# Sigmoid attention over 96x96 images: two key chunks per step of the attention loop instead of three

## The chip, the cores and the metric

The kernel runs on one core of a Trainium2 chip. A core has a matrix engine (TensorE, PE in the profile; its weight loads are listed as PEld), a vector engine (VectorE, DVE), an engine for activation functions (ScalarE, ACT), a general one (GpSimd, POOL) and one that mostly issues DMA transfers (SyncE, SP). The engines run their own instruction queues in order and wait for one another through semaphores. TensorE writes its results into PSUM, a memory of eight banks, each 512 fp32 numbers wide per partition; ScalarE and VectorE read them from there.

The metric is the device time of one execution in microseconds (us).

## The reference

The input x has the shape (4, 64, 96, 96): four images b, 64 channels, N = 9216 positions. Two layers are applied, each to a group-normalized copy of x and added to x:

```python
Q = (wq @ gn(x) + bq)          # 8 channels, per image
K = (wk @ gn(x) + bk)          # 8 channels
V = (wv @ gn(x) + bv)          # 64 channels
energy = einsum('bcn,bcm->bnm', Q, K)        # 9216 x 9216 per image
att = sigmoid(energy)
out = einsum('bcm,bnm->bcn', V, att) + gn(x)
x = x + out * channel_gate(out)              # gate from mean and maximum of each channel
# second layer: a spectral convolution with few frequencies
x = x + irfft2(lowpass_mix(rfft2(gn(x))))
```

There is no softmax: the attention matrix is a sigmoid of each energy, so the sum over keys m can be cut into chunks of any size.

## The kernel before

**Tiling.** Two images form a pair: 2 x 64 channels fill the 128 partitions. The loop over p runs over the two pairs. Positions are cut in blocks of NB = 512 (NBLK = 18) for queries, and in chunks of P = 128 (NCH = 72) for keys.

**Per pair.** First come group statistics (`group_stats`) and then the projection of keys and values: for each of the 18 blocks s, VectorE normalizes 512 columns (`normalize`, L135), TensorE computes the keys (L163, one matmul) and the transposed values (L166, four matmuls) into one PSUM tile `proj`, ScalarE makes two copies of the keys with bias (L171, L172), VectorE joins these into `kT` (L177, four instructions, one for each key chunk) and copies the values into `vT` (L180). The keys stand four times in the 128 partitions, as four groups of 32 rows: two images, times two.

**The attention loop.** For each query block n an accumulator `acc` in PSUM is summed over all keys. A step t takes three key chunks, so there are NT = 24 steps in a block. `energies(n, t, q)` issues six matmuls (L207): three chunks times two images, each with 32 rows of weights from `kT` and 512 query columns from `q`. The row group of a matmul is r = 32 * (2 * (m % 2) + b), so that the first four matmuls use four different groups and the last two use the first two groups again. The results fill two PSUM tiles of three banks each. ScalarE applies the sigmoid to each tile with one instruction of 1536 columns (L212) and writes `at` to SBUF. `values(acc, t, ats)` issues six matmuls (L220) with 64 columns of weights, one image in each half of the array's columns; the profile lists twelve records for them, as each is done in two passes. In the program order the energies of step t + 1 stand ahead of the values of step t, so that ScalarE can work meanwhile.

**Queries.** `project_q(n + 1)` (L191, then L195 to L197 on VectorE) is called after the values of step NT - 3 of block n; its result is first used by the energies that are issued in step NT - 1.

**Buffers.** PSUM: pool `ps_s` has two slots of three banks, used by `proj` and by the energies `e`; pool `ps_a` has two slots of one bank for `acc`, `pq` and small things. In SBUF the pool `att` has four slots for `at` and, in the projection, `kk` (the two copies of the keys); the pool `q` holds `q`, `qh` and `ql`. With these slots the first energies of a step wait until the first sigmoid of the step before has read its PSUM tile, and the fourth energy matmul waits for the second sigmoid.

**After the loop** the channel gate is computed, x is updated (L265), and after the second pair the spectral stage follows. Its four constant matrices fw, fh, gh and gw are loaded by ScalarE's DMA queue at its start (L280 to L283).

The order of the work on each engine follows the program text, except that a scheduler moves independent instructions, such as the normalization of later blocks, forward or back.

Of the kernel before, what the change touches and what calls it, by code (L numbers as in the profile page):

```python
# [13 lines left out]
F32 = mybir.dt.float32  # L14
F32R = mybir.dt.float32r
AF = mybir.ActivationFunctionType
ALU = mybir.AluOpType
AX = mybir.AxisListType
PSUM = bass.MemoryType.PSUM

P = 128
B, C, H, W = 4, 64, 96, 96
# [4 lines left out]
KW = 16  # L27
KH = 32
NB = 512
NBLK = N // NB  # L30
NCH = N // P
NT = NCH // 3
WKH = 2
GN_EPS = 1e-5

# [2 lines left out]
def tile_kernel(ctx: ExitStack, tc: tile.TileContext, x, wqT, bq, wkT, bk, wvT, bv,  # L38
                w1T, w2T, spec, fw, fh, gh, gw, pairavg, halves, out):
    nc = tc.nc  # L40
# [3 lines left out]
    const = ctx.enter_context(tc.tile_pool(name="const", bufs=1))  # L44
# [40 lines left out]
    q_low, q_sign, k_low, k_sign = (hv[:, i:i + 1] for i in range(4))  # L85
# [10 lines left out]
    for b in range(2):  # L96
# [2 lines left out]
        nc.scalar.dma_start(w2_sb[b * R:(b + 1) * R, b * C:(b + 1) * C], w2T)  # L99
        nc.scalar.dma_start(bv_sb[:, b, :], bv.to_broadcast([P, C]))  # L100

    turn = [0]

    def evacuate(dst, src):
# [29 lines left out]
    def normalize(dst, src, mr):  # L134
        nc.vector.tensor_scalar(dst, src, mr[:, 0:1], mr[:, 1:2], ALU.subtract, ALU.mult)  # L135
# [4 lines left out]
    with tc.tile_pool(name="xn", bufs=1) as xnp, \  # L140
            tc.tile_pool(name="kv", bufs=1) as kvp, \
            tc.tile_pool(name="q", bufs=2) as qp, \
            tc.tile_pool(name="att", bufs=4) as attp, \
            tc.tile_pool(name="ps_s", bufs=2, space=PSUM) as ps_s, \
            tc.tile_pool(name="ps_a", bufs=2, space=PSUM) as ps_a:
        for p in range(NPAIR):
            xt = xs[p]
# [5 lines left out]

            xn = xnp.tile([P, N], F32, tag="xn", name=f"xn_{p}")


            kT = kvp.tile([P, NT, 2, P], F32R, tag="kT", name=f"kT_{p}")
            vT = kvp.tile([P, NCH, P], F32, tag="vT", name=f"vT_{p}")
            for s in range(NBLK):
                cols = bass.ts(s, NB)  # L160
                normalize(xn[:, cols], xt[:, cols], mr)
                pp = ps_s.tile([P, 3, NB], F32, tag="s", name=f"proj_{p}_{s}")
                nc.tensor.matmul(pp[:, 0, :], wk_sb, xn[:, cols], start=True, stop=True)  # L163
                for i in range(4):
                    j = 4 * s + i
                    nc.tensor.matmul(pp[:, 1, bass.ts(i, P)], xn[:, bass.ts(j, P)], wv_sb,  # L166
                                     start=True, stop=True)

                kk = attp.tile([P, 3, NB], F32, tag="att", name=f"kk_{p}_{s}")
                kh, kl = kk[:, 0, :].bitcast(F32R), kk[:, 1, :]  # L170
                nc.scalar.activation(kh, pp[:, 0, :], AF.Identity, bias=bk_sb[:, 0:1])  # L171
                nc.scalar.activation(kl, pp[:, 0, :], AF.Identity, bias=bk_sb[:, 1:2],  # L172
                                     scale=k_low)
                for i in range(4):
                    t, m = (4 * s + i) // 3, (4 * s + i) % 3
                    rows = slice(64 * (m % 2), 64 * (m % 2) + 64)
                    nc.vector.scalar_tensor_tensor(  # L177
                        kT[rows, t, m // 2, :], kk[rows, 0, bass.ts(i, P)],
                        k_sign[rows, :], kl[rows, bass.ts(i, P)], ALU.mult, ALU.add)
                nc.vector.tensor_tensor(  # L180
                    vT[:, 4 * s:4 * s + 4, :],
                    pp[:, 1, :].rearrange("p (i m) -> p i m", m=P),
                    bv_sb.rearrange("p b c -> p (b c)").unsqueeze(1).to_broadcast([P, 4, P]),
                    ALU.add)
# [4 lines left out]
            def project_q(n):  # L189
                pq = ps_a.tile([P, NB], F32, tag="a", name=f"pq_{p}_{n}")  # L190
                nc.tensor.matmul(pq, wq_sb, xn[:, bass.ts(n, NB)], start=True, stop=True)  # L191
                qh = qp.tile([P, NB], F32R, tag="hi", bufs=1, name=f"qh_{p}_{n}")
                ql = qp.tile([P, NB], F32, tag="lo", bufs=1, name=f"ql_{p}_{n}")
                q = qp.tile([P, NB], F32R, tag="q", name=f"q_{p}_{n}")
                nc.vector.tensor_scalar(qh, pq, bq_sb[:, 0:1], None, ALU.add)  # L195
                nc.vector.tensor_scalar(ql, pq, bq_sb[:, 0:1], q_low, ALU.add, ALU.mult)
                nc.vector.scalar_tensor_tensor(q, qh.bitcast(F32), q_sign, ql, ALU.mult, ALU.add)  # L197
                return q

            def energies(n, t, q):  # L200

                es = [ps_s.tile([P, 3, NB], F32, tag="s", name=f"e_{p}_{n}_{t}_{i}")
                      for i in range(2)]
                for i in range(6):
                    m, b = i // 2, i % 2
                    r = 32 * (2 * (m % 2) + b)
                    nc.tensor.matmul(es[i // 3][:, i % 3, :], kT[r:r + 32, t, m // 2, :],  # L207
                                     q[r:r + 32, :], start=True, stop=True)
                ats = []
                for i in range(2):  # L210
                    at = attp.tile([P, 3, NB], F32, tag="att", name=f"at_{p}_{n}_{t}_{i}")
                    nc.scalar.activation(at, es[i], AF.Sigmoid)  # L212
                    ats.append(at)
                return ats

            def values(acc, t, ats):
                for i in range(6):
                    j, b = 3 * t + i // 2, i % 2
                    half = slice(b * C, (b + 1) * C)
                    nc.tensor.matmul(acc[half, :], vT[:, j, half], ats[i // 3][:, i % 3, :],  # L220
                                     start=(j == 0), stop=(j == NCH - 1))

            q = project_q(0)
            ats = energies(0, 0, q)
            for n in range(NBLK):
                acc = ps_a.tile([P, NB], F32, tag="a", name=f"acc_{p}_{n}")
                for t in range(NT):
                    nxt = None
                    if t + 1 < NT:
                        nxt = energies(n, t + 1, q)  # L230
                    elif n + 1 < NBLK:
                        nxt = energies(n + 1, 0, q)
                    values(acc, t, ats)
                    ats = nxt
                    if t == NT - 3 and n + 1 < NBLK:
                        qn = project_q(n + 1)
                    if t == NT - 2 and n + 1 < NBLK:
                        q = qn
                blk = xn[:, bass.ts(n, NB)]
                nc.vector.scalar_tensor_tensor(blk, acc, 1.0, blk, ALU.mult, ALU.add,  # L240
                                               accum_out=sums[:, n:n + 1])
                nc.vector.tensor_reduce(maxs[:, n:n + 1], blk, AX.X, ALU.max)


            f = small.tile([P, 2], F32, tag="f", name=f"f_{p}")
# [25 lines left out]
    with tc.tile_pool(name="big", bufs=1) as big, \  # L271
            tc.tile_pool(name="wspec", bufs=3) as wp, \
            tc.tile_pool(name="strip", bufs=3) as sp, \
            tc.tile_pool(name="ps1", bufs=8, space=PSUM) as ps:

        fw_sb = big.tile([W, 3 * KW], F32, tag="fw", name="fw_sb")
        fh_sb = big.tile([H, 2, 3 * KH], F32, tag="fh", name="fh_sb")
        gh_sb = big.tile([2 * KH, H], F32, tag="gh", name="gh_sb")
        gw_sb = big.tile([2 * KW, W], F32, tag="gw", name="gw_sb")
        nc.scalar.dma_start(fw_sb, fw)  # L280
        nc.scalar.dma_start(fh_sb, fh)
        nc.scalar.dma_start(gh_sb, gh)
        nc.scalar.dma_start(gw_sb, gw)  # L283

        def bank(name):
            return ps.tile([P, NB], F32, tag="b", name=name)
# [4 lines left out]
        for p in range(NPAIR):  # L291
# [12 lines left out]
            a = big.tile([H, 2, KW, 3, C], F32, tag="t24", name=f"a_{p}")  # L304
            for g in range(P // 8):
                pa = bank(f"pa_{p}_{g}")
                for i in range(8):
                    nc.tensor.matmul(pa[:H, bass.ts(i, 3 * KW)], xT[:, :, 8 * g + i], fw_sb,  # L308
                                     start=True, stop=True)
                b, c0 = 8 * g // C, 8 * g % C  # L310
# [21 lines left out]
        for g in range(KH // WKH):  # L332
            wt = wp.tile([P, WKH, KW, C], F32, tag="wt", name=f"wt_{g}")
            nc.sync.dma_start(wt.rearrange("q h k o -> q (h k o)"), spec[g])
            for i in range(WKH):
                kh = WKH * g + i
                pv = bank(f"pv_{kh}")
                for kw in range(KW):
                    nc.tensor.matmul(pv[:C, bass.ts(kw, 3 * B)], wt[:, i, kw, :],  # L339
                                     u[:, kh, kw, :, :].rearrange("q s b -> q (s b)"),  # L340
                                     start=True, stop=True)
# [3 lines left out]
        for p in range(NPAIR):  # L345
# [16 lines left out]
            for g in range(P // 4):  # L362
                pz = bank(f"pz_{p}_{g}")
                for i in range(4):
                    b, o = (4 * g + i) // C, (4 * g + i) % C
                    nc.tensor.matmul(pz[:2 * KW, bass.ts(i, H)],  # L366
                                     vt[:, b, :, :, o].rearrange("q e k -> q (e k)"), gh_sb,
                                     start=True, stop=True)
# [69 lines left out]
```

## Time and profile before

| | us |
|---|---|
| median of 3 runs | 3665.22 |
| lowest and highest run | 3664.88, 3665.68 |
| the profiled execution, its own time | 3665.68 |
| span of its profile, first to last instruction | 3663.9 |
| TensorE busy in the span | 3510.7 |
| ScalarE busy | 2535.0 |
| VectorE busy | 408.2 |
| sigmoids (L212), 1728 of 1448 ns | 2412.3 |
| values (L220), records of TensorE | 2419.8 |
| energies (L207), records of TensorE | 635.4 |
| key and value projection (L163, L166), records of TensorE | 83.3 |

The page's busy times are sums over the whole program. A matmul's record lasts from its start until its result is out, so that records of following matmuls overlap: a mean of 601 ns for a value matmul doesn't mean that TensorE needs 601 ns for each. The distance from one start to the next is what counts, and it is read from the timeline.

In time order the program has five parts: loading and statistics until 33 us; projection and attention of pair 0 until 1594; gate, update and statistics until 1621; projection and attention of pair 1 until 3160; gate, update and the spectral stage until the end.

### The profile page before, as it was taken

To read this page: it belongs to the slowest core of one execution; us is meant where nothing else is said; L and a number is where in the kernel's file an instruction comes from. 1 tells how busy PE (TensorE), PEld (TensorE's weight loads), DVE (VectorE), ACT (ScalarE), POOL (GpSimd) and SP (SyncE) were. 2 spreads that over 40 slices of the span, in tenths; PEclk is the share of its full clock that TensorE was granted. 3 is DMA by queue.
4 is the path that set the end of the run, shared out by engine and by line. 5 is a ranking of instruction groups with operands and counts; after the bars stand their busy time and mean duration, and the time that the engine had idled before them with its cause. 6 is when DMAs were issued, how large, how long until landed. Compare 5 with 4: busy or idle time off the path is not lost.

```text
span 3663.9 us, 42847 instructions
## 1 busy us (share of the span) xinstructions
PE 3510.7 (96%) x19016; PEld 1439.6 (39%) x19016; DVE 408.2 (11%) x778; ACT 2535.0 (69%) x1908; POOL 2.9 (0%) x10
## 2 busy tenths in 40 slices
PE   3999999999999999968999999999999999699999
PEld 2333333333333333323333333333333333289999
DVE  6100000000000000052000000000000000431032
ACT  1788888888888888847888888888888888411011
POOL 0000000000000000000000000000000000000000
PEclk9999999999999999989999999999999999855555
DMA  3000000000000000000000000000000000000311
GB/s 106 1 1 1 1 1 1 1 1 1 1 1 1 1 1 1 1 1 1 1 1 1 1 1 1 1 1 1 1 1 1 1 1 1 36 1 24 127 52 52
DMA packets 9705, 38.75 MB, mean 11 GB/s; under 512 B 4689, under 2 KB 4913, under 8 KB 6449
## 3 DMA queue, kind: packets, MB, share of 16 engines
q1 hardware_dynamic: 5184, 35.65, 2.7%
q8 instruction: 149, 2.44, 0.3%
q10 hardware_dynamic: 4336, 0.37, 0.1%
q14 instruction: 36, 0.29, 0.0%
HBM read 26.58 MB, written 9.44 MB: 10 GB/s over the span
## 4 chain that ended last, share of the span: by engine, by line
PE 53%; DVE 1%; issue 0%; ACT 0%; POOLq 0%; POOL 0%; DVEq 0%
PE acc L220 32%; PE e L207 8%; PE pv L339 3%; PE pa L308 2%; PE py L375 2%; PE pz L366 2%; PE pu L320 1%; PE pu L323 1%; PE pq L191 0%; DVE strip L135 0%; PE pvt L353 0%; DVE x L265 0%; DVE stats L113 0%; PE pt L300 0%; DVE xT L108 0%
## 5 line engine op out<-in xcount | busy, mean ns | idle before, releaser
L212 ACT ACTIVATE at<-e 128x1536 f32<-128x1536 f32 x1728 | 2412.3, 1448 | 554.8 <-PE e L207 553.1
L220 PE MATMUL acc<-at,vT 128*64 128x512 f32 x10368 | 2419.8, 601 | 0.0
L220 PEld LDWEIGHTS acc<-at,vT 128*64 128x64 f32 x10368 | 668.3, 136 | 1306.3 <-issue 1306.3
L207 PE MATMUL e<-q,kT 32*128 32x512 f32 x5184 | 635.4, 461 | 6.7 <-DVE vT L180 6.1
L207 PEld LDWEIGHTS e<-q,kT 32*128 32x128 f32 x5184 | 256.3, 182 | 707.3 <-issue 480.4
L195 DVE TENSOR_SCALAR qh<-pq,wqb 128x512 fp32r<-128x512 f32 x36 | 27.0, 750 | 2533.3 <-PE pq L191 2533.3
L339 PE MATMUL pv<-u,wt 128*64 128x12 f32 x1024 | 109.4, 261 | 0.0
L339 PEld LDWEIGHTS pv<-u,wt 128*64 128x64 f32 x1024 | 109.3, 227 | 0.2 <-issue 0.2
L308 PE MATMUL pa<-fw_sb,xT 96*96 96x48 f32 x512 | 84.5, 361 | 1.3 <-ACT xT L110 1.3
L308 PEld LDWEIGHTS pa<-fw_sb,xT 96*96 96x96 f32 x512 | 84.2, 257 | 1.8 <-ACT xT L110 1.8
L163 PE MATMUL proj<-xn,wk 128*128 128x512 f32 x72 | 43.1, 686 | 43.3 <-DVE vT L180 19.8
L375 PE MATMUL py<-gw_sb,z 32*128 32x96 f32 x384 | 82.5, 417 | 1.8 <-ACT z L110 1.8
L375 PEld LDWEIGHTS py<-gw_sb,z 32*128 32x128 f32 x384 | 82.1, 328 | 2.4 <-ACT z L110 2.4
L366 PE MATMUL pz<-gh_sb,vt 64*32 64x96 f32 x512 | 82.3, 364 | 0.0
L366 PEld LDWEIGHTS pz<-gh_sb,vt 64*32 64x32 f32 x512 | 81.6, 174 | 0.3 <-issue 0.3
L171 ACT ACTIVATE kk<-proj,wkb 128x512 fp32r<-128x512 f32 x36 | 24.7, 687 | 79.7 <-PE proj L166 38.8
L110 ACT COPY v<-pv 64x192 f32<-64x192 f32 x16 | 7.6, 477 | 101.4 <-PE pv L339 101.4
L110 ACT COPY z<-pz 32x384 f32<-32x384 f32 x32 | 25.4, 795 | 57.2 <-PE pz L366 57.2
L110 ACT COPY a<-pa 96x384 f32<-96x384 f32 x16 | 12.8, 799 | 73.5 <-PE pa L308 73.5
L240 DVE SCALAR_TENSOR_TENSOR xn<-acc,xn 128x512 f32<-128x512 f32 x36 | 24.9, 692 | 312.2 <-PE acc L220 312.2
L177 DVE SCALAR_TENSOR_TENSOR kT<-kk,hv 64x128 fp32r<-64x128 f32 x144 | 46.9, 345 | 26.1 <-ACT kk L172 24.7
L128 PE MATMUL pv_l<-t_l,pav 128*128 128x1 f32 x8 | 2.3, 359 | 49.3 <-DVE t_l L126 49.3
(68 smaller groups left out, 765.4 us busy)
## 6 DMA issues: line engine op xcount, KB each, us to landing
wt<-in_spec_dram SPq DMA_DIRECT2D x16, 1024.0 KB
x<-in_x_dram SPq DMA_DIRECT2D x8, 1152.0 KB
out_dram<-x SPq DMA_DIRECT2D x12, 768.0 KB
wq<-in_wqT_dram ACTq DMA_DIRECT2D x16, 2.0 KB
wqb<-in_bq_dram ACTq DMA_DIRECT2D x16, 0.0 KB
wk<-in_wkT_dram ACTq DMA_DIRECT2D x16, 2.0 KB
wkb<-in_bk_dram ACTq DMA_DIRECT2D x16, 0.0 KB
fh_sb<-in_fh_dram ACTq DMA_DIRECT2D x1, 72.0 KB
```

The lines of the kernel that those rows point to most:

```text
L110: nc.scalar.copy(dst, src)
L163: nc.tensor.matmul(pp[:, 0, :], wk_sb, xn[:, cols], start=True, stop=True)
L177: nc.vector.scalar_tensor_tensor(kT[rows, t, m // 2, :], kk[rows, 0, bass.ts(i, P)], k_sign[rows, :], kl[rows, bass.ts(i, P)], ALU.mult, A ...
L207: nc.tensor.matmul(es[i // 3][:, i % 3, :], kT[r:r + 32, t, m // 2, :], q[r:r + 32, :], start=True, stop=True)
L212: nc.scalar.activation(at, es[i], AF.Sigmoid)
L220: nc.tensor.matmul(acc[half, :], vT[:, j, half], ats[i // 3][:, i % 3, :], start=(j == 0), stop=(j == NCH - 1))
L308: nc.tensor.matmul(pa[:H, bass.ts(i, 3 * KW)], xT[:, :, 8 * g + i], fw_sb, start=True, stop=True)
L320: nc.tensor.matmul(o, a[:, b, kw, 1:3, :].rearrange("h s c -> h (s c)"), fh_sb[:, 0, :], start=True, stop=False)
L323: nc.tensor.matmul(o, a[:, b, kw, 0:2, :].rearrange("h s c -> h (s c)"), fh_sb[:, 1, :], start=False, stop=True)
L339: nc.tensor.matmul(pv[:C, bass.ts(kw, 3 * B)], wt[:, i, kw, :], u[:, kh, kw, :, :].rearrange("q s b -> q (s b)"), start=True, stop=True)
L366: nc.tensor.matmul(pz[:2 * KW, bass.ts(i, H)], vt[:, b, :, :, o].rearrange("q e k -> q (e k)"), gh_sb, start=True, stop=True)
L375: nc.tensor.matmul(py[:, bass.ts(i, W)], z[:, 4 * g + i, :], gw_sb, start=True, stop=True)
```

## The change

A step of the attention loop takes two key chunks instead of three, so there are 36 steps in a query block instead of 24. `energies` issues four matmuls, one for each row group, into two PSUM tiles of two banks; a sigmoid has 1024 columns instead of 1536, and there are three where there were two; `values` issues four matmuls. The pool `ps_s` has three slots of two banks instead of two of three, six banks in both cases.

The layout of `kT` follows: chunk j = 2 jj + i stands in rows 64 i to 64 i + 63. VectorE therefore joins the keys of a block with two instructions of 64x256 instead of four of 64x128, and `kh` and `kl` come from the pool `q` under the tags of `qh` and `ql`, with two slots each, instead of from `att`. In the scheduled order, the instructions that make q of block 0 on VectorE come at the end of the projection (the first of them ahead of the last block's kT, the other two behind its vT); before, they came at its start. `project_q(n + 1)` is still called after the third last step and first used by the energies issued in the last step.

The four constants of the spectral stage move to the pool `const` and are loaded at the program's start, on ScalarE's queue behind the weights.

```diff
+    fw_sb = const.tile([W, 3 * KW], F32, tag="fw", name="fw_sb")
...
+    nc.scalar.dma_start(fw_sb, fw)
...
-            tc.tile_pool(name="ps_s", bufs=2, space=PSUM) as ps_s, \
+            tc.tile_pool(name="ps_s", bufs=3, space=PSUM) as ps_s, \
...
-            kT = kvp.tile([P, NT, 2, P], F32R, tag="kT", name=f"kT_{p}")
+            kT = kvp.tile([P, NCH // 2, P], F32R, tag="kT", name=f"kT_{p}")
...
-                pp = ps_s.tile([P, 3, NB], F32, tag="s", name=f"proj_{p}_{s}")
+                pp = ps_s.tile([P, 2, NB], F32, tag="s", name=f"proj_{p}_{s}")
...
-                kk = attp.tile([P, 3, NB], F32, tag="att", name=f"kk_{p}_{s}")
-                kh, kl = kk[:, 0, :].bitcast(F32R), kk[:, 1, :]
+                kh = qp.tile([P, NB], F32R, tag="hi", name=f"kh_{p}_{s}")
+                kl = qp.tile([P, NB], F32, tag="lo", name=f"kl_{p}_{s}")
...
-                for i in range(4):
-                    t, m = (4 * s + i) // 3, (4 * s + i) % 3
-                    rows = slice(64 * (m % 2), 64 * (m % 2) + 64)
-                    nc.vector.scalar_tensor_tensor(
-                        kT[rows, t, m // 2, :], kk[rows, 0, bass.ts(i, P)],
-                        k_sign[rows, :], kl[rows, bass.ts(i, P)], ALU.mult, ALU.add)
+                for e in range(2):
+                    rows = slice(64 * e, 64 * e + 64)
+                    hh, ll = (a[rows, :].rearrange("p (a e m) -> p a e m", e=2, m=P)[:, :, e, :]
+                              for a in (kh.bitcast(F32), kl))
+                    nc.vector.scalar_tensor_tensor(kT[rows, 2 * s:2 * s + 2, :], hh,
+                                                   k_sign[rows, :], ll, ALU.mult, ALU.add)
...
-                for i in range(6):
-                    m, b = i // 2, i % 2
-                    r = 32 * (2 * (m % 2) + b)
-                    nc.tensor.matmul(es[i // 3][:, i % 3, :], kT[r:r + 32, t, m // 2, :],
-                                     q[r:r + 32, :], start=True, stop=True)
+                for i in range(2):
+                    for b in range(2):
+                        r = 32 * (2 * i + b)
+                        nc.tensor.matmul(es[i][:, b, :], kT[r:r + 32, jj, :], q[r:r + 32, :],
+                                         start=True, stop=True)
...
-                    at = attp.tile([P, 3, NB], F32, tag="att", name=f"at_{p}_{n}_{t}_{i}")
+                    at = attp.tile([P, 2, NB], F32, tag="att", name=f"at_{p}_{n}_{jj}_{i}")
...
-                for i in range(6):
-                    j, b = 3 * t + i // 2, i % 2
-                    half = slice(b * C, (b + 1) * C)
-                    nc.tensor.matmul(acc[half, :], vT[:, j, half], ats[i // 3][:, i % 3, :],
-                                     start=(j == 0), stop=(j == NCH - 1))
+                for i in range(2):
+                    j = 2 * jj + i
+                    for b in range(2):
+                        half = slice(b * C, (b + 1) * C)
+                        nc.tensor.matmul(acc[half, :], vT[:, j, half], ats[i][:, b, :],
+                                         start=(j == 0), stop=(j == NCH - 1))
...
-                for t in range(NT):
+                for jj in range(NCH // 2):
...
-                    if t == NT - 3 and n + 1 < NBLK:
+                    if jj == NCH // 2 - 3 and n + 1 < NBLK:
                         qn = project_q(n + 1)
-                    if t == NT - 2 and n + 1 < NBLK:
+                    if jj == NCH // 2 - 2 and n + 1 < NBLK:
                         q = qn
...
-        fw_sb = big.tile([W, 3 * KW], F32, tag="fw", name="fw_sb")
...
-        nc.scalar.dma_start(fw_sb, fw)
```

More of the change, by code (lines that the diff above doesn't have):

```diff
@@ L31 @@
 NCH = N // P
-NT = NCH // 3
 WKH = 2
@@ L100, in tile_kernel @@
         nc.scalar.dma_start(bv_sb[:, b, :], bv.to_broadcast([P, C]))
+    fw_sb = const.tile([W, 3 * KW], F32, tag="fw", name="fw_sb")
+    fh_sb = const.tile([H, 2, 3 * KH], F32, tag="fh", name="fh_sb")
+    gh_sb = const.tile([2 * KH, H], F32, tag="gh", name="gh_sb")
+    gw_sb = const.tile([2 * KW, W], F32, tag="gw", name="gw_sb")
+    nc.scalar.dma_start(fw_sb, fw)
+    nc.scalar.dma_start(fh_sb, fh)
+    nc.scalar.dma_start(gh_sb, gh)
+    nc.scalar.dma_start(gw_sb, gw)
     turn = [0]
@@ L191, in project_q @@
                 nc.tensor.matmul(pq, wq_sb, xn[:, bass.ts(n, NB)], start=True, stop=True)
-                qh = qp.tile([P, NB], F32R, tag="hi", bufs=1, name=f"qh_{p}_{n}")
-                ql = qp.tile([P, NB], F32, tag="lo", bufs=1, name=f"ql_{p}_{n}")
+                qh = qp.tile([P, NB], F32R, tag="hi", name=f"qh_{p}_{n}")
+                ql = qp.tile([P, NB], F32, tag="lo", name=f"ql_{p}_{n}")
                 q = qp.tile([P, NB], F32R, tag="q", name=f"q_{p}_{n}")
@@ L198, in project_q, with energies @@
                 return q
-            def energies(n, t, q):
-                es = [ps_s.tile([P, 3, NB], F32, tag="s", name=f"e_{p}_{n}_{t}_{i}")
+            def energies(n, jj, q):
+                es = [ps_s.tile([P, 2, NB], F32, tag="s", name=f"e_{p}_{n}_{jj}_{i}")
                       for i in range(2)]
-                for i in range(6):
-                    m, b = i // 2, i % 2
-                    r = 32 * (2 * (m % 2) + b)
-                    nc.tensor.matmul(es[i // 3][:, i % 3, :], kT[r:r + 32, t, m // 2, :],
-                                     q[r:r + 32, :], start=True, stop=True)
+                for i in range(2):
[3 more added lines that the diff above has]
+                                         start=True, stop=True)
                 ats = []
                 for i in range(2):
-                    at = attp.tile([P, 3, NB], F32, tag="att", name=f"at_{p}_{n}_{t}_{i}")
+                    at = attp.tile([P, 2, NB], F32, tag="att", name=f"at_{p}_{n}_{jj}_{i}")
                     nc.scalar.activation(at, es[i], AF.Sigmoid)
@@ L214, in energies, with values @@
                 return ats
-            def values(acc, t, ats):
-                for i in range(6):
-                    j, b = 3 * t + i // 2, i % 2
-                    half = slice(b * C, (b + 1) * C)
-                    nc.tensor.matmul(acc[half, :], vT[:, j, half], ats[i // 3][:, i % 3, :],
-                                     start=(j == 0), stop=(j == NCH - 1))
+            def values(acc, jj, ats):
+                for i in range(2):
[4 more added lines that the diff above has]
+                                         start=(j == 0), stop=(j == NCH - 1))
             q = project_q(0)
@@ L226, in tile_kernel @@
                 acc = ps_a.tile([P, NB], F32, tag="a", name=f"acc_{p}_{n}")
-                for t in range(NT):
+                for jj in range(NCH // 2):
                     nxt = None
-                    if t + 1 < NT:
-                        nxt = energies(n, t + 1, q)
+                    if jj + 1 < NCH // 2:
+                        nxt = energies(n, jj + 1, q)
                     elif n + 1 < NBLK:
                         nxt = energies(n + 1, 0, q)
-                    values(acc, t, ats)
+                    values(acc, jj, ats)
                     ats = nxt
-                    if t == NT - 3 and n + 1 < NBLK:
+                    if jj == NCH // 2 - 3 and n + 1 < NBLK:
                         qn = project_q(n + 1)
-                    if t == NT - 2 and n + 1 < NBLK:
+                    if jj == NCH // 2 - 2 and n + 1 < NBLK:
                         q = qn
@@ L274, in tile_kernel @@
             tc.tile_pool(name="ps1", bufs=8, space=PSUM) as ps:
-        fw_sb = big.tile([W, 3 * KW], F32, tag="fw", name="fw_sb")
-        fh_sb = big.tile([H, 2, 3 * KH], F32, tag="fh", name="fh_sb")
-        gh_sb = big.tile([2 * KH, H], F32, tag="gh", name="gh_sb")
-        gw_sb = big.tile([2 * KW, W], F32, tag="gw", name="gw_sb")
-        nc.scalar.dma_start(fw_sb, fw)
-        nc.scalar.dma_start(fh_sb, fh)
-        nc.scalar.dma_start(gh_sb, gh)
-        nc.scalar.dma_start(gw_sb, gw)
         def bank(name):
```

## The prediction

> **What bounds the kernel now.** I read four views in this order: the page's busy times and groups, the table by stretches, the timeline of one step of the attention loop, and the timeline where that loop begins.
>
> ```profile
> PE 3510.7 (96%) x19016; PEld 1439.6 (39%) x19016; DVE 408.2 (11%) x778; ACT 2535.0 (69%) x1908; POOL 2.9 (0%) x10
> L212 ACT ACTIVATE at<-e 128x1536 f32<-128x1536 f32 x1728 | 2412.3, 1448 | 554.8 <-PE e L207 553.1
> ...
> 187.00:1580.00 1393.00, 1393.00 (x7340) 438.39 (x7341) 61.32 (x102) 1132.92 (x812) 0.00 (x0) 1.00 0.00 1
> ```
>
> The last line is the steady loop of the first pair: us, then busy PE, PEld, DVE, ACT. TensorE has no gap and a full clock, ScalarE is busy 81%, and what ScalarE waits for is TensorE. So the loop's time is TensorE's.
>
> One step of it (three key chunks), as merged rows: start, us, engine.
>
> ```profile
> 1501.56 0.73 PE L207 MATMUL e<-q,kT 32*128 32x512 f32 x6
> 1501.90 0.40 PE L207 MATMUL e<-q,kT 32*128 32x512 f32 x2
> 1502.17 2.79 ACT L212 ACTIVATE at<-e 128x1536 f32<-128x1536 f32 x2 [0.60 <-PE e L207]
> 1502.23 2.79 PE L220 MATMUL acc<-at,vT 128*64 128x512 f32 x12
> 1502.71 0.14 PEld L220 LDWEIGHTS acc<-at,vT 128*64 128x64 f32 x2 [0.28 <-issue]
> 1503.14 0.14 PEld L220 LDWEIGHTS acc<-at,vT 128*64 128x64 f32 x2 [0.28 <-issue]
> ...
> 1504.95 1.13 PE L191 MATMUL pq<-xn,wq 128*128 128x512 f32 x2
> 1505.48 0.59 PE L191 MATMUL pq<-xn,wq 128*128 128x512 f32 x1
> 1506.12 0.75 DVE L195 TENSOR_SCALAR qh<-pq,wqb 128x512 fp32r<-128x512 f32 x1 [74.18 <-PE pq L191]
> 1507.62 0.75 DVE L197 SCALAR_TENSOR_TENSOR q<-qh,hv,ql 128x512 fp32r<-128x512 f32 x1
> ```
>
> The six energy matmuls go in two waves, four row groups at 1501.56 and two at 1501.90; the values begin at 1502.23. Over 860 steps the trace's stamps give 0.663 us from energies to values and 2.726 us from values to whatever follows: 3.389 us. The values are six pairs: the first takes 0.48 us, the next ones 0.429 each (a weight load stands at each pair's start), and the last is followed after 0.528.
>
> At the loop's first steps there is an energy wave that stands alone, three matmuls, at half the clock (a value pair lasts 0.91 us there, 112.16 to 113.07):
>
> ```profile
> 108.81 0.79 PE L207 MATMUL e<-q,kT 32*128 32x512 f32 x3 [0.62 <-ACT at L212]
> 109.54 1.97 PE L220 MATMUL acc<-at,vT 128*64 128x512 f32 x2
> 111.44 0.80 PE L207 MATMUL e<-q,kT 32*128 32x512 f32 x3
> 112.16 3.46 PE L220 MATMUL acc<-at,vT 128*64 128x512 f32 x10
> 113.07 0.24 PEld L220 LDWEIGHTS acc<-at,vT 128*64 128x64 f32 x2 [0.62 <-issue]
> ```
>
> Before each loop stands the projection of keys and values, 18 blocks per pair, where TensorE waits:
>
> ```profile
> 66.25 1.10 PE L163 MATMUL proj<-xn,wk 128*128 128x512 f32 x2 [1.75 <-DVE vT L180]
> 68.09 1.10 PE L163 MATMUL proj<-xn,wk 128*128 128x512 f32 x2
> 68.32 0.69 ACT L171 ACTIVATE kk<-proj,wkb 128x512 fp32r<-128x512 f32 x1 [2.43 <-issue]
> 69.71 1.34 DVE L177 SCALAR_TENSOR_TENSOR kT<-kk,hv 64x128 fp32r<-64x128 f32 x4 [1.76 <-ACT kk L172]
> 71.92 1.10 PE L163 MATMUL proj<-xn,wk 128*128 128x512 f32 x2 [1.84 <-DVE vT L180]
> ```
>
> Two blocks in 5.67 us: a PSUM slot comes free only after ScalarE and VectorE are through, and there are two slots.
>
> **What the skill says.** "TensorEngine Tiling (Array Packing)", Key Properties: a change of tiling mode drains the array. The trace agrees: 0.528 - 0.429 = 0.10 us are lost from values (column tiles) to energies (row tiles). "TensorE: Matmul & The Clock Gate", LDWEIGHTS: a load takes its columns over 1.2 GHz, 107 ns for 128, 53 for 64. Where nothing hides it the trace shows this too: pq's first pass takes 0.534 against 0.429 (0.105 for 128 columns), a step's first value pair 0.480 (0.051 for 64). Same page, Part 3: tiles of different row groups run together; the four of a wave start within 10 ns. "ScalarE: Activation LUTs", What ACT_TABLE_LOAD costs: 0.833 ns an element. One ACTIVATE of 1536 starts 1.347 us after the one before it, so one of 1024 is estimated at 1.347 - 0.427 = 0.92.
>
> **The change, part by part.**
>
> *The loop's step.* Two chunks instead of three: one wave of four energies, four value pairs. Values: 0.480 + 2x0.429 + 0.528 = 1.866. The wave alone isn't in the trace at full clock with four row groups. From above: take a wave's stream off the two-wave step. It is 0.335 (wave to wave) less the load's 0.105, or 0.326 (wave 2 to values) less a drain of 0.10: 0.23; with half a value pair, 0.213. So 0.663 - 0.213 = 0.450, or 0.433. From below: the lone wave at half clock took 0.724. If all of it went with the clock it would be 0.362; but the load and drain don't halve fully (pq's load is 0.158 there, 34.225 - 33.212 less 0.855; value to energy is 0.989, only 0.461 over 0.528), which leaves 0.724 - 0.213 - 0.053 - 0.033 = 0.425. I take 0.435, as two of three ways say so. Step: 2.301 for two chunks, against 3.389 x 2/3 = 2.259. The second wave hid its weight load and shared one pair of drains with three chunks; now two chunks pay them. 2 pairs x 18 blocks x 36 steps = 1296: 1296 x 0.042 = **+54 us** (ends: 0.362 gives -43, 0.450 gives +74).
>
> *ScalarE* has 2 x 0.92 = 1.84 us per 2.30, hidden. The third slot decouples it: the second energy pair waits for the first sigmoid of the step before, which ends some 0.61 + 1.02 = 1.6 us into a step of 2.30; the values' second half waits for the second sigmoid, which ends at 2.55 and is wanted at 2.30 + 0.44 + 0.91 = 3.65. Energies' wait on TensorE itself is for a wave two steps back. Nothing queues.
>
> *q of the next block.* It is still begun two steps before use, but steps are shorter. q ends 3.42 us after pq starts (1504.95 to 1508.37), plus about 0.1 to reach TensorE. The energies that use it come after pq, a wave and the values: 1.056 + 0.435 + 1.866 = 3.36 (before: 4.45, free). 34 stalls x 0.15 = **+5 us** (0 to 8); TensorE's whole queue stands behind it.
>
> *Projection.* Three slots, and two kT instructions of 64x256 instead of four of 64x128. At 344 ns for 128 elements and 1.04 per further one (the 128x512 row, 751 ns, fits) two take about 0.93 us instead of 1.33. A slot's round falls from 5.67 to 5.27 us and three share it: 1.76 a block. TensorE needs 1.84 (66.25 to 68.09) and binds. The kh and kl buffers, two each, come free within that. Gain about 16 x (2.80 - 1.84) = 15 us per pair. Against it: q of block 0, finished early before, now stands behind the last vT on VectorE (0.7 + 0.75 us, and its first instruction ahead of the last kT, 0.7); TensorE then idles 4 to 5 us, and the loop starts at half clock. Before, that also cost 1.6 to 3.3 us (block start at 105.4 and 1674.2, steady loop as if from 108.7 and 1675.7), so I charge 1 us. In pair 1 seven normalizations of 0.46 lie between the kT on VectorE, 2 us more. Pair 0: -13, pair 1: -11: **-24 us** (-17 to -30).
>
> *Constants moved.* Four DMA issues of about 0.5 us (the neighbouring rows of the same queue) go before ScalarE's table load: the first kk would be 0.7 us late, taken into pair 0. They no longer stand before the spectral stage's copies on that queue, where the copies wait 28 us for TensorE anyway: 0 to -1, I take -0.5. Gate, statistics and spectral stage keep their instructions and order.
>
> Sum: 54 + 5 - 24 - 0.5 = +35 on the profiled execution's 3665.7 us (span 3663.9 and 1.8 around it), which is the highest of three; on the median of 3665.2, **3700 us**.
>
> **Rivals.** (1) *Faster: the lone wave is cheap.* If load and drain go with the clock, the wave takes 0.362, a step 2.228; 1296 x -0.031 = -40, stalls +8, projection -24: -57, 3608 us. It decides below a wave of about 0.409, where the loop's loss no longer outweighs the projection's gain. For it: three chunks' 0.724 halved. Against: pq's exposed load. (2) *The projection gives less*, because VectorE's order or half-clock stretches take back what slots give (-8), and the wave is 0.450: +74 + 5 - 8 = +71, 3736 us. For it: the half clock seen at both starts of the loop. (3) *ScalarE becomes the bound*: if a step's waves wait for the last sigmoid, a step is 0.61 + 0.92 + 1.02 = 2.55, 1296 x 0.29 = +376, 4017 us (with the projection's gain). Against: the third slot and the waits above. (4) *The two effects cancel*: wave 0.41, within 7 us.
>
> **How the numbers follow.** Forecast 0.55 (+10 to +55 us: 3675 to 3720); rival 1 0.16; rival 2 0.18; rival 3 0.04; rival 4 0.07. This kernel's measurement can tell 0.2% (7 us) from no change. Slower: 0.55 + 0.18 + 0.04 = 0.77. The range 3655 to 3738 leaves out about 0.14 below and 0.06 above.
>
> **What would show it.** In the steady loop, an energies-to-values distance of 0.43 to 0.45 with one wave, values-to-energies of 1.87, ScalarE some 80% busy; a wait of energies for VectorE's q, 34 times 0.1 to 0.2 us; key projections every 1.85 us with no wait for vT. Wrong: a step under 2.26 us, a wait of energies or values for sigmoids in every step, or projections still 2.8 us apart.

## The result and the profile after

The kernel after takes 3704.43 us (median of 4 runs, 3703.25 to 3705.2) against 3665.05 us (4 runs, 3664.02 to 3665.68): 1.0107 times as long, 95% interval 1.009 to 1.0125. That is +39.4 us; +35 had been forecast.

The page of the kernel after: span, busy times, the chain that ended last, and the three groups of the attention loop (count | busy us, mean ns | idle before it, ended by whom).

```profile
span 3703.4 us, 44494 instructions
...
PE 3566.7 (96%) x19016; PEld 1392.4 (38%) x19016; DVE 397.1 (11%) x706; ACT 2634.5 (71%) x2772; POOL 2.9 (0%) x10
...
PE acc L228 65%; PE e L214 15%; PE pv L338 3%; PE pa L307 2%; PE py L374 2%; PE pz L365 2%; DMA x<-in_x_dram 1%; PE pq L198 1%; PE proj L170 1%; PE proj L173 1%; PE pu L319 1%; PE pu L322 1%; DVE x L273 1%; DVE stats L121 1%; DVE strip L143 0%
...
L219 ACT ACTIVATE at<-e 128x1024 f32<-128x1024 f32 x2592 | 2512.1, 1021 | 528.9 <-PE e L214 527.3
L228 PE MATMUL acc<-at,vT 128*64 128x512 f32 x10368 | 2514.0, 606 | 0.0
...
L214 PE MATMUL e<-q,kT 32*128 32x512 f32 x5184 | 659.8, 497 | 15.8 <-DVE q L204 9.8
```

TensorE has the same 19016 matmul records, and ScalarE still waits for energies. The 864 sigmoids more add 99.8 us to ScalarE's busy time, which still leaves it 29% to spare. So the loss must be looked for between TensorE's starts.

The same stretch of the steady loop of pair 0 in the table by stretches (us, then busy PE, PEld, DVE, ACT, with counts):

```profile
187.00:1580.00 1393.00, 1390.84 (x7180) 407.82 (x7176) 57.71 (x96) 1154.88 (x1192) 0.00 (x0) 1.00 0.00 1
```

Before, this stretch held 7340 matmuls with TensorE busy for all of it. Now it holds 7180, 2.2% fewer, and 2.2 us are idle. The clock is full in both. Each step costs more, and a little is waited for. The timeline of two steps (start, us, engine):

```profile
1500.44 0.51 PE L214 MATMUL e<-q,kT 32*128 32x512 f32 x4
...
1500.88 1.94 PE L228 MATMUL acc<-at,vT 128*64 128x512 f32 x8
1501.04 1.94 ACT L219 ACTIVATE at<-e 128x1024 f32<-128x1024 f32 x2 [0.37 <-PE e L214]
...
1502.74 0.51 PE L214 MATMUL e<-q,kT 32*128 32x512 f32 x4
...
1503.18 1.94 PE L228 MATMUL acc<-at,vT 128*64 128x512 f32 x8
```

One wave of four energies, 0.437 us to the values (median of 1292 steps by the trace's stamps), and 1.868 us from the values to the next energies: 2.305 us for two chunks, where 2.259 was the share of two chunks before. Over 1296 steps that is +59.2 us (with 2.2593 for the share before). Blocks start 84.23 us apart, 82.39 before.

Where a block changes its q:

```profile
259.99 1.12 PE L198 MATMUL pq<-xn,wq 128*128 128x512 f32 x2
...
261.49 1.94 PE L228 MATMUL acc<-at,vT 128*64 128x512 f32 x8
...
262.66 0.75 DVE L204 SCALAR_TENSOR_TENSOR q<-qh,hv,ql 128x512 fp32r<-128x512 f32 x1
...
263.56 0.51 PE L214 MATMUL e<-q,kT 32*128 32x512 f32 x4
```

From the values at 261.49 to the energies at 263.56 are 2.07 us instead of 1.868: q ends at 263.41, and the energies follow it. There are 34 of these stalls of 0.206 us, +7.0 us in all. No line of the waits names them: TensorE's wait for q is listed there with 9.8 us and 2 times, at the starts of the two loops. In the stall shown, 0.07 us lies under the record of the values, which ends at 263.43; the other 0.13 (34 x 0.13 = 4.4 us) is in the 15.8 us of idle time in the energies' group, with no releaser named. The distance between starts shows the whole.

The projection, and the first energies of pair 0:

```profile
64.30 1.02 PE L170 MATMUL proj<-xn,wk 128*128 128x512 f32 x2
...
66.05 1.02 PE L170 MATMUL proj<-xn,wk 128*128 128x512 f32 x2
...
91.88 0.75 DVE L204 SCALAR_TENSOR_TENSOR q<-qh,hv,ql 128x512 fp32r<-128x512 f32 x1
...
92.78 1.22 PE L214 MATMUL e<-q,kT 32*128 32x512 f32 x6 [5.32 <-DVE q L204]
```

From the sixth on, blocks of pair 0's projection are 1.75 to 1.81 us apart with no wait for vT, 2.84 before. In pair 1, where VectorE still has seven normalizations to do, some are 2.06 apart, and the mean from the second block on is 1.87. Then TensorE stands 5.3 us for q of block 0 (4.5 in pair 1). The start of each loop is reckoned back from its steady blocks to where its first energies would stand. By this reckoning the loop starts 13.7 us earlier than before in pair 0, and the stretch between the loops is 12.4 us shorter: -26.1 us.

Loop +59.2 and +7.0 (the spans of both loops, from the first energies to the last values' start, give +65.9), projections -26.1: +39.8 with the spans of the loops, against +39.5 in the spans of the two profiles.

### The profile page after: what moved, and what is told of

It is laid out like the page before. It is cut to its first block, busy times and chain, and to the rows that moved or that the text cites. A ratio compares the mean times of both kernels' runs of the same rounds, so it can differ in the third digit from the quotient of the medians.

```text
span 3703.4 us, 44494 instructions
## 1 busy us (share of the span) xinstructions
PE 3566.7 (96%) x19016; PEld 1392.4 (38%) x19016; DVE 397.1 (11%) x706; ACT 2634.5 (71%) x2772; POOL 2.9 (0%) x10
## 4 chain that ended last, share of the span: by engine, by line
PE 94%; DVE 3%; DMA 1%; issue 0%; ACT 0%; ACTq 0%; POOL 0%; POOLq 0%; DVEq 0%
PE acc L228 65%; PE e L214 15%; PE pv L338 3%; PE pa L307 2%; PE py L374 2%; PE pz L365 2%; DMA x<-in_x_dram 1%; PE pq L198 1%; PE proj L170 1%; PE proj L173 1%; PE pu L319 1%; PE pu L322 1%; DVE x L273 1%; DVE stats L121 1%; DVE strip L143 0%
## 5 line engine op out<-in xcount | busy, mean ns | idle before, releaser
L219 ACT ACTIVATE at<-e 128x1024 f32<-128x1024 f32 x2592 | 2512.1, 1021 | 528.9 <-PE e L214 527.3
L228 PE MATMUL acc<-at,vT 128*64 128x512 f32 x10368 | 2514.0, 606 | 0.0
L228 PEld LDWEIGHTS acc<-at,vT 128*64 128x64 f32 x10368 | 629.4, 136 | 1062.3 <-issue 1061.2
L214 PE MATMUL e<-q,kT 32*128 32x512 f32 x5184 | 659.8, 497 | 15.8 <-DVE q L204 9.8
L178 ACT ACTIVATE kh<-proj,wkb 128x512 fp32r<-128x512 f32 x36 | 24.7, 687 | 46.4 <-PE proj L173 44.8
L118 ACT COPY xT<-pt 96x512 f32<-96x512 f32 x24 | 14.0, 582 | 51.7 <-PE pt L299 51.7
```

What stands on the lines that cost most here:

```text
L118: nc.scalar.copy(dst, src)
L214: nc.tensor.matmul(es[i][:, b, :], kT[r:r + 32, jj, :], q[r:r + 32, :], start=True, stop=True)
L228: nc.tensor.matmul(acc[half, :], vT[:, j, half], ats[i][:, b, :], start=(j == 0), stop=(j == NCH - 1))
```

## The experiments

The first four kernels, and those with four kT instructions and with late constants, change one part of the kernel after; the last two build on the first. A difference of times is between medians. One under 7 us is relied on only where a trace shows it too.

**Three chunks per step, all else as after.**

```
+G = 3
-            tc.tile_pool(name="att", bufs=4) as attp, \
+            tc.tile_pool(name="att", bufs=6) as attp, \
...
-                for i in range(2):
+                for i in range(G):
+                    j = G * t + i
...
-                        r = 32 * (2 * i + b)
-                        nc.tensor.matmul(es[i][:, b, :], kT[r:r + 32, jj, :], q[r:r + 32, :],
+                        r = 32 * (2 * (j % 2) + b)
+                        nc.tensor.matmul(es[i][:, b, :], kT[r:r + 32, j // 2, :], q[r:r + 32, :],
```

> The kernel after with three chunks per step instead of two: three two-bank energy tiles, three sigmoids of 1024 per step, 24 steps per block; projection, kT layout, q buffers and constants as after. Theory A (a step costs TensorE a fixed 0.36 to 0.38 us over its streams, whatever the number of chunks in it: exposed weight loads and the drains of two mode switches): the step is 3.39 us again, steady blocks 82.4 us instead of 84.2, loop -66 us over both pairs, and the projection's gain of 26 us stays: 3638 us (3632 to 3645), faster than both kernels. Rival B (the loss comes from the smaller sigmoids, 1024 instead of 1536 elements): blocks stay at 84.2 us, 3704 us.

3644.5 us (5 runs), 0.9945 times before, interval 0.9932 to 0.9957. Its timeline:

```profile
1503.10 0.73 PE L216 MATMUL e<-q,kT 32*128 32x512 f32 x6
1503.70 2.85 ACT L221 ACTIVATE at<-e 128x1024 f32<-128x1024 f32 x3 [0.53 <-PE e L216]
...
1503.76 2.79 PE L230 MATMUL acc<-at,vT 128*64 128x512 f32 x12
...
1506.49 0.73 PE L216 MATMUL e<-q,kT 32*128 32x512 f32 x6
```

The step is 3.39 us again, with sigmoids of 1024: what the loop lost was the number of chunks in a step, not the sigmoids' size. The total is 6 us above the forecast: the stretch between the loops is only 9.4 us shorter than before's instead of 12.4, and some blocks of pair 0 take 82.55 us instead of 82.39. The reasons were not tried. For the first, the trace shows that pair 1's first block takes 87.10 us where before's takes 85.35; that three tiles have to be filled from three slots there is a likely cause.

**One chunk per step**, with q begun early enough not to be waited for.

```
+G = 1
...
-                    if jj == NCH // 2 - 3 and n + 1 < NBLK:
+                    if jj == NCH // G - 6 and n + 1 < NBLK:
```

> The kernel after with one chunk per step: one energy tile and one sigmoid of 1024 per step, 72 steps per block, two row groups in a wave; q of the next block is begun six steps before it is used, so that nothing waits for it. Theory A (fixed cost per step): energies to values 0.437, values 0.480 + 0.528 = 1.008, step 1.445 us per chunk against 1.152 now; 2592 x 0.2925 = +758, less 6.5 of q's stall: 4456 us. Rival B (the size of the sigmoids makes the loss, and that is unchanged): 3698 us. If a wave of two row groups costs less than one of four, between the two: 2592 x what it is cheaper by.

4445.64 us (2 runs).

```profile
1501.22 0.50 PE L216 MATMUL e<-q,kT 32*128 32x512 f32 x2
...
1501.65 1.08 PE L230 MATMUL acc<-at,vT 128*64 128x512 f32 x4
1501.81 1.02 ACT L221 ACTIVATE at<-e 128x1024 f32<-128x1024 f32 x1 [0.41 <-PE e L216]
...
1502.66 0.50 PE L216 MATMUL e<-q,kT 32*128 32x512 f32 x2
```

Energies to values 0.430 us, values 1.009: 1.439 for one chunk. A wave of two row groups costs 0.430 and one of four 0.437, so that leaving two of the four row groups empty saves almost nothing; the 0.007 over 2592 steps are 18 us less than forecast, the main reason why 741 us were added and not 752. The three kernels together (streams: 0.429 for a value pair, half of it for a wave, which is an estimate):

| chunks in a step | step, us | value pairs and waves | streams, us | the rest, us |
|---|---|---|---|---|
| 1 | 1.439 | 2 and 1 | 1.072 | 0.367 |
| 2 | 2.305 | 4 and 1 | 1.930 | 0.375 |
| 3 | 3.389 | 6 and 2 | 3.003 | 0.386 |

The rest hardly depends on the step's size. On the values' side this needs no estimate: 1.009, 1.868 and 2.726 us less 0.429 for each pair leave 0.151, 0.152 and 0.152. On the energies' side it rests on the estimated stream. "TensorEngine Tiling (Array Packing)", Key Properties, in the Trainium skill says that switching the tiling mode drains the array; each step switches twice, from row tiles to column tiles and back, and each switch is followed by a weight load. A cost per pair of switches, whatever the work between them, is what the three kernels show. How the 0.375 divide between drains and loads was not tried by itself; by the prediction's pieces it is 0.10 and 0.051 on the values' side and 0.437 - 0.2145 = 0.22 on the energies'.

**The next q one step earlier.**

```
-                    if jj == NCH // 2 - 3 and n + 1 < NBLK:
+                    if jj == NCH // 2 - 4 and n + 1 < NBLK:
```

> The kernel after with the query projection of the next block begun one step earlier (three steps before use instead of two). Theory A: the wait of the energies for q at each block's start, about 0.19 us in the trace after, is real and goes, 34 x 0.19 = 6.5 us: 3698 us, blocks 84.05 instead of 84.23. Rival B: the stall only takes the place of another wait, 3704 us as before.

3697.34 us (5 runs, 3696.79 to 3697.54), 7.1 less than after, and blocks of 84.03 us. In the traces the two loops together are 7.0 us shorter, which is 34 times 0.206. The stall was real and nothing took its place.

**Two energy slots instead of three.**

```
-            tc.tile_pool(name="ps_s", bufs=3, space=PSUM) as ps_s, \
+            tc.tile_pool(name="ps_s", bufs=2, space=PSUM) as ps_s, \
```

> The kernel after with two energy slots of PSUM instead of three, so that only the slots are undone. Theory A: the third slot alone gives most of the projection's gain (blocks 2.6 us apart instead of 1.75, +14 us per pair) and keeps ScalarE off the path in the loop: with two slots the second energy pair waits for the second sigmoid of the step before, a step is about 2.6 us, 1296 x 0.3 = +390: 4120 us in all (4050 to 4200). Rival B (TensorE sets the step with two slots also): loop unchanged, only the projection's +28: 3732 us.

3911.68 us (2 runs): +207, between the two theories. The projections gave 28.7 us back, by the same reckoning of the starts, and their blocks are 2.65 us apart, as forecast. The loop gave 178, less than half of what was expected. Its timeline:

```profile
1500.34 0.47 PEld L214 LDWEIGHTS e<-q,kT 32*128 32x128 f32 x4 [0.81 <-ACT at L219]
1500.34 0.79 PE L214 MATMUL e<-q,kT 32*128 32x512 f32 x4
1500.94 1.94 ACT L219 ACTIVATE at<-e 128x1024 f32<-128x1024 f32 x2 [0.36 <-PE e L214]
...
1501.06 1.94 PE L228 MATMUL acc<-at,vT 128*64 128x512 f32 x8
...
1502.92 0.50 PE L214 MATMUL e<-q,kT 32*128 32x512 f32 x4
...
1503.36 1.94 PE L228 MATMUL acc<-at,vT 128*64 128x512 f32 x8
1503.53 1.94 ACT L219 ACTIVATE at<-e 128x1024 f32<-128x1024 f32 x2 [0.65 <-PE e L214]
...
1505.22 0.80 PE L214 MATMUL e<-q,kT 32*128 32x512 f32 x4
```

Longer and shorter steps alternate. From 1500.34 the second pair of energies waits for a sigmoid (the wave lasts 0.79), and the step takes 2.58; from 1502.92 it doesn't wait (0.50), and the step takes 2.30. The forecast had this step (2.6) and put it on all of them. But a late second pair makes its own step longer while the first pair and its sigmoid were in time, so that ScalarE has caught up by the next step. The two steps shown are the extreme: over the whole loop the medians of the longer and the shorter steps are 2.51 and 2.38 us, and blocks of 89.27 us (pair 0) and 89.07 (pair 1) against 84.23 make 0.14 us a step, half of what 2.58 shows. A wait worked out from one step need not stay in a steady state; it has to be followed over two. The third slot is worth some 180 us in the loop and 29 in the projections.

**Four kT instructions instead of two.**

```
-                    hh, ll = (a[rows, :].rearrange("p (a e m) -> p a e m", e=2, m=P)[:, :, e, :]
-                              for a in (kh.bitcast(F32), kl))
-                    nc.vector.scalar_tensor_tensor(kT[rows, 2 * s:2 * s + 2, :], hh,
-                                                   k_sign[rows, :], ll, ALU.mult, ALU.add)
+                    for g in range(2):
+                        cc = bass.ts(2 * g + e, P)
+                        nc.vector.scalar_tensor_tensor(kT[rows, 2 * s + g, :], kh[rows, cc].bitcast(F32),
+                                                       k_sign[rows, :], kl[rows, cc], ALU.mult, ALU.add)
```

> The kernel after with four kT instructions of 64x128 per projection block again instead of two of 64x256; three slots stay. Theory A: VectorE then has 1.34 + 0.72 = 2.06 us per block, more than TensorE's 1.76, and binds: blocks 2.06 to 2.1 us apart, +0.3 x 17 = +5 us per pair: 3714 us (3709 to 3718). Rival B: the third slot alone makes the gain (vT of the block three back is what matters) and the kT are hidden: 3704 us, blocks 1.76 apart.

3713.1 us (4 runs): 8.7 more.

```profile
65.42 0.69 DVE L189 TENSOR_TENSOR vT<-proj,bv 128x512 f32<-128x512 f32 x1
66.02 1.23 DVE L185 SCALAR_TENSOR_TENSOR kT<-kh,hv,kl 64x128 fp32r<-64x128 f32 x4
...
67.28 0.69 DVE L189 TENSOR_TENSOR vT<-proj,bv 128x512 f32<-128x512 f32 x1
67.89 1.23 DVE L185 SCALAR_TENSOR_TENSOR kT<-kh,hv,kl 64x128 fp32r<-64x128 f32 x4
```

VectorE has no gap and sets the pace, as theory A said, but at 1.87 us a block, not 2.06: four kT take 1.23 us here, not the 1.34 of before. The stamps of the two traces show why. A kT instruction that writes the same half of the partitions as the one ahead of it starts 0.26 to 0.27 us after that one; where the half changes, 0.35 to 0.37 us after it. This holds for all 216 starts within the blocks of both kernels. Of the three starts in a block, two change the half in the kernel before, and one here. Why a change costs more is not shown. By the reckoning of the starts, four instructions cost 0.9 us in pair 0, and 6.0 in pair 1, where VectorE has the normalizations too. So of the projection's 26 us the merged kT are worth about 7 to 9 once the slots are there; each change alone leaves the other's limit.

**The spectral constants loaded late again.**

```
-    fw_sb = const.tile([W, 3 * KW], F32, tag="fw", name="fw_sb")
...
-    nc.scalar.dma_start(fw_sb, fw)
...
+        fw_sb = big.tile([W, 3 * KW], F32, tag="fw", name="fw_sb")
...
+        nc.scalar.dma_start(fw_sb, fw)
```

> The kernel after with the four spectral constants loaded in the spectral stage again. Theory A: no effect that the measurement can tell, 3704 us within 2 us, since nothing waits for them at either place: in the trace the first kh comes at the end of the table load within 0.5 us of its place now, and the stretch from the last values to the end stays 504 us. Rival B: the four issues ahead of the table load delay the first kh by 2 us: the first kh comes at 53.8 instead of 55.8, 3702 us.

3703.35 us (4 runs, 3702.5 to 3703.8). The 1.1 us to after are too little to tell by the times. In its trace the table load comes right behind the last issue for bv, and the first kh 1.4 us earlier than the 55.83 of after:

```profile
52.30 1.28 ACT L169 ACT_TABLE_LOAD   x1 [52.30 <-DMA wv<-in_wvT_dram]
...
53.01 2.29 PE L164 MATMUL proj<-wv,xn 128*128 128x128 f32 x16 [0.33 <-DMA wv<-in_wvT_dram]
54.45 0.69 ACT L169 ACTIVATE kh<-proj,wkb 128x512 fp32r<-128x512 f32 x1 [0.86 <-PE proj L164]
```

kh waits for TensorE's projection here, not for its table. Neither theory had its number: between these two traces kh differs by 1.4 us, not 2 and not under 0.5. The last experiment's kernel, with late constants too, has its table load at 52.03 and kh at 54.77; the seven kernels with early constants have it at 55.63 or later. So the early loads do delay kh. They are no gain of the change; a cost of about 1 us in all is likely and not shown. (In the two single traces the loop of pair 0 starts 2.8 us earlier here, but after's projection has a stretch of half clock from 59.63 to 63.04 that this one lacks.)

**Buffers of their own for q.** In the kernel of the first experiment the key projection takes its buffers from the att pool again, and q is free of it.

```
-                kh = qp.tile([P, NB], F32R, tag="hi", name=f"kh_{p}_{s}")
-                kl = qp.tile([P, NB], F32, tag="lo", name=f"kl_{p}_{s}")
+                kk = attp.tile([P, 2, NB], F32, tag="att", name=f"kk_{p}_{s}")
+                kh, kl = kk[:, 0, :].bitcast(F32R), kk[:, 1, :]
...
+                qh = qp.tile([P, NB], F32R, tag="hi", bufs=1, name=f"qh_{p}_{n}")
```

> The kernel of e1 (three chunks per step, three slots of two banks) with the buffers of the key projection taken from the att pool again, so that qh and ql have buffers of their own and q of block 0 is finished early instead of behind the last kT on VectorE. Theory A: the 5.3 us in which TensorE waits for q at the loop's start go, the energies begin with the last projections and the first sigmoid comes when its table is loaded (89.5 us instead of 92.9 in pair 0): -3.4 us per pair, a little more if the clock stays up: 3637 us (3633 to 3641). Rival B: the loop's start is set by the last vT and the half clock anyway, 3643 to 3645.

3640.52 us (5 runs, 3638.14 to 3642.04), 4 less than with shared buffers (3643.68 to 3644.88). That is little for the times alone, but the trace puts it where it was expected: pair 0's loop starts about 4 us earlier. Pair 0:

```profile
86.39 0.50 PE L216 MATMUL e<-q,kT 32*128 32x512 f32 x2
...
87.92 1.28 ACT L221 ACT_TABLE_LOAD   x1
...
89.22 2.99 ACT L221 ACTIVATE at<-e 128x1024 f32<-128x1024 f32 x3
```

The first sigmoid comes at the end of its table load, at 89.22. In the first experiment it came at 92.85, and waited for the energies:

```profile
92.85 2.86 ACT L221 ACTIVATE at<-e 128x1024 f32<-128x1024 f32 x3 [3.39 <-PE e L216]
```
Pair 1 did not change: the scheduler had put that pair's first query projection behind the last projection of keys and values, and TensorE still waits 4.5 us for q there:

```profile
1640.16 1.02 PE L199 MATMUL pq<-xn,wq 128*128 128x512 f32 x2
...
1645.67 1.22 PE L216 MATMUL e<-q,kT 32*128 32x512 f32 x6 [4.48 <-DVE q L205]
...
1649.26 1.97 PE L230 MATMUL acc<-at,vT 128*64 128x512 f32 x2
```

**The query projection moved in the program.**

```
+                if s == 0:
+                    q = project_q(0)
...
-            q = project_q(0)
```

The first two lines stand at the end of the projection's loop; the constants are loaded late.

> The kernel of e5, with the query projection of block 0 put behind the first key projection in the program, so that it runs early in pair 1 as well (in e5 its matmul came last there, and TensorE waited 4.5 us for q), and with the spectral constants loaded late as in e7. Theory A: pair 1's loop starts some 3.5 us earlier as pair 0's did in e5, and the first kh of pair 0 about 1.4 us earlier: 3640.5 - 3.5 - 1.2 = 3636 us (3632 to 3639). Rival B: with q early VectorE only does its work at another time while it is the busier engine in pair 1 (normalizations, kT, vT), so that the loop starts no earlier: 3639 to 3641.

3633.49 us (5 runs, 3632.09 to 3633.59), 7.0 less than the kernel it builds on and 0.9914 times before, interval 0.9901 to 0.9928: the fastest kernel here. Pair 1:

```profile
1640.70 0.50 PE L209 MATMUL e<-q,kT 32*128 32x512 f32 x2
...
1642.10 2.85 ACT L214 ACTIVATE at<-e 128x1024 f32<-128x1024 f32 x3
...
1643.61 1.07 PE L223 MATMUL acc<-at,vT 128*64 128x512 f32 x2
```

The stretch between the loops shrinks by 5.2 us where 3.5 had been expected. The first two values have a record of 1.07 us, where the kernel without this edit had 1.97. TensorE no longer stands still for q, and the clock differs too: the trace's granted clock is half from 1644.94 to 1648.35 here, 3.4 us, and from 1645.65 to 1655.89 there, 10.2 us.

## Why the prediction was right

The sign, and the terms of its sum, held; none was off by more than 6 us. The experiments undid the step, the wait for q and the parts of the projection one by one, and each moved the time by about its term.

| step of the prediction | forecast | measured |
|---|---|---|
| wave that stands alone | 0.435 us | 0.437 |
| values of a step | 1.866 us | 1.868 |
| step, over 1296 | +54 us | +59.2 |
| wait for q, 34 times | 0.15 us, +5 | 0.206 us, +7.0 |
| projections | -24 us | -26.1 |
| first kh late by the constants | 0.7 us | about 1.4 (single traces) |

- *The loop's step.* The choice of 0.435 between 0.362 and 0.450 decided the sign, and the wave's cost proved almost what the subtractions gave. That it was met within 0.002 us is partly luck: the three ways gave 0.425, 0.433 and 0.450, and 0.01 us of it are 13 us in the sum. 0.004 us in a step, 1296 times, are the 5 us by which the sum fell short. Rival 1, the cheap wave, would have needed less than 0.409.
- *ScalarE hidden.* Right, and for the reason named: with two slots the energies do wait for sigmoids. Rival 3's step of 2.55 is near the longest steps of the two-slot kernel (2.58), but there a shorter step follows each longer one, and the mean is 2.45.
- *The wait for q.* Right in place and cause, mis-sized by 0.05 us: q ends 0.15 us before the energies that use it start, where about 0.1 had been taken.
- *Projection.* The round of a slot (5.27 us forecast, two blocks in 5.31 measured with two slots) was right. TensorE's own need was taken as 1.84 us a block from a place before where two blocks followed each other; with three slots it is 1.75. The slots would not have given it alone: without the merged kT, VectorE binds at 1.87. The 2 us more that were charged for pair 1's normalizations are seen as well: blocks 1.87 us apart there on the mean.
- *q of block 0 behind the last vT.* The 4 to 5 us of idling were 5.3 and 4.5. The net charge of 1 us for it was a comparison with before; against a kernel without it, it costs some 4 us in pair 0 and 5 in pair 1. That is what the loops' starts gained in the last two experiments.
- *Constants.* The first kh came at 55.83 against 55.78 before, so that the forecast delay seems absent. The two kernels with late constants show it (54.45 and 54.77). In the trace of before, kh was late for another reason: the first matmuls with wv, which kh waits for when its table is ready, began at 53.79 instead of 53.12, and 16 of them took 2.85 us instead of 2.02.
- *Slips in the working.* None moves the sum by more than 2 us. The four energies of a wave do not all start within 10 ns in the kernel before: in 96% of its steps the fourth starts later, about 0.06 us after the first. After the change the four do start within 10 ns. It is not shown why. The end of 0.362 is given with -43 at one place and -40 at another (-41 is right). Pair 1's terms add up to -12, where -11 was written; the measured -12.4 is nearer to their sum.

## What to carry to other kernels

Where an engine alternates between two modes, count what a step pays once, and divide by the work in it: here a step paid 0.37 to 0.39 us whether it held one chunk, two or three, and three won although their second wave is half empty. A change that bundles a loss in the loop with gains around it is worth taking apart: the kernel with three chunks and the change's three slots and merged instructions beats both. Freeing a buffer does not by itself make a result early: in pair 0 it did, in pair 1 nothing changed until the producer was moved in the program as well (moving it alone was not tried). Check the order on every pass of the outer loop.

## What was not expected of the hardware

- A wave of two row groups takes as long as one of four: 0.430 and 0.437 us from its start to the values.
- A missing slot costs half of what one step shows: longer and shorter steps alternate, 2.58 and 2.30 us at the extreme, and the loss is 0.14 us a step.
- Four VectorE instructions of 64x128 take 1.23 us in one order and 1.34 in another: the next one starts 0.26 to 0.27 us after the last within one half of the partitions, 0.35 to 0.37 where the half changes.
- Among the kernels that load the constants early, whose programs begin alike, the first kh stands anywhere from 55.63 to 56.73 us in the trace: a difference of a microsecond between two single spans can't be read as an effect of the change.
